# Two attention layers on one core: scores of layer 1 by differences, projections in fewer gaps, a later product on GpSimd, and additions shared with VectorE in one block

## The chip, the core and the metric

The kernel runs on one NeuronCore of a Trainium2 chip. The metric is the device time of one execution in microseconds (us). TensorE is called PE in the profile, its weight loads PEld, VectorE DVE, ScalarE ACT, GpSimd POOL, and SP is the queue that starts most of the transfers.

## The reference, cut to what matters

```python
# x: (2, 256, 64, 64) float32, n = 64*64 = 4096 positions
def layer0(x, w_qkv, w_proj):            # 8 heads of 32 channels
    q, k, v = split(einsum('oc,bcn->bon', w_qkv, x), 3)
    scores = einsum('bhdi,bhdj->bhij', q, k) / sqrt(32)
    out = einsum('bhij,bhdj->bhdi', softmax(scores, axis=-1), v)
    return einsum('oc,bcn->bon', w_proj, out) + x

def layer1(x):                           # one head, keys and values pooled to 1024 positions
    g = maxpool2(conv1x1(x, g_w, g_b))                  # 256 channels x 1024
    theta = conv1x1(x[:, :64], theta_w, theta_b)        #  64 channels x 4096
    phi = maxpool2(conv1x1(x[:, 64:], phi_w, phi_b))    #  64 channels x 1024
    f = softmax(einsum('bcn,bcm->bnm', theta, phi), axis=-1)
    y = einsum('bnm,bcm->bcn', f, g)
    return batchnorm(conv1x1(y, W_w, W_b)) + x
```

Both layers are done in float32 for each of the two batches; each row of a softmax has its largest score subtracted before the exponential.

## The kernel before

**Layer 0.** Four heads are done together, so there are four groups `n` (two batches, two quads of heads), and each has 8 blocks `i` of 512 queries: 32 blocks in all, counted 0 to 31 below. A block has 32 steps `j`, one for each tile of 128 keys. In a step PE makes the scores of the four heads (`score`, L401), and ACT takes the exponential of two heads at a time (L530) into `p`. Even steps start the scores' buffer in PSUM from the negated row maxima (`subtract`, L413: matmuls of `ones_b` with `rows`, in bfloat16); odd steps add the product of the queries with differences of keys (`kd`, `last_kd`) to the scores that still stand there. One step later `weigh` multiplies the probabilities with the values (L425), and DVE adds that to `num` (L436).

**The denominator.** `add` sums the probabilities over the steps: heads 0 and 1 (`p[0]`, 128x1024) on POOL (L449), heads 2 and 3 two steps at a time by accumulating transfers that POOL issues (L457), in turn into two sums. The tiles of `p[0]` come from a pool of 6 buffers, the double tiles of `p[1]` from a pool of 5; ACT can write a tile only when its addition or its transfer is done with it. In the following block `normalize` runs as a generator, a piece a step: a last accumulating transfer at step 2 (L463), the column sums on PE at step 6 (`den`, L475) and their copy by ACT to `r` (L483), two transfers through DRAM from step 7 on (L492, L493), the reciprocal of step 12 (L497), the transfers that spread it over the partitions again (L498, L500), and, five pieces later, at step 17, the product `y = num * r` on POOL (L505). The last block of a batch takes another way: ACT's copy, a reciprocal on DVE (L486) and the product.

**Row maxima.** They are found ahead by a second set of products (`product`, L252), of which two are made at each half step (`advance(maxes)`). DVE reduces them, directly (L264) or together with differences that ACT has cut at zero (L271, L278). This work is one block and some steps ahead: at step 28 of block i it begins with the queries of block i + 2.

**Projections in the gaps.** `during` lists what is projected in a block: for most blocks the queries of block i + 2, and keys and values of chunk i for the next group. One item is made in each of the steps 11, 19 and 27, after that step's `weigh`: `make` reads a chunk of `x` (one buffer), PE multiplies (L195 for q and k, L183 for v), and ACT copies the result out of PSUM (L209, L192). The PSUM tiles for these, for `w` and for the products of the maxima come from one pool of 4 banks (`scratch`); the scores take the other two buffers of two banks each (`scores`). In group 3 there is no next group, and only the queries are left.

**Layer 1.** `project` (L559) ends layer 0 for a batch. `non_local` makes `theta`, `phi` and `g`, folds the output matrix into the values (`wg`), and then goes through 8 blocks `i` of 512 queries with 4 steps `t` of 256 keys. In each step PE makes the scores (L719) and adds the negated maxima (L728, bfloat16), ACT takes the exponential (L732), PE weighs the step before (L687), POOL sums the probabilities (L679, L683), and PE makes a piece of the maxima of later blocks (L655) that DVE reduces (L662). `result` ends a block: column sums (L699), reciprocal (L701) and two pairs of operations on DVE (L703, L706).

Each engine works through its own queue in order; the framework sets the semaphores, and it may let an instruction with ready operands pass others of the program's order.

Of the kernel before, what the change touches and what calls it, by code (L numbers as in the profile page):

```python
# [9 lines left out]
F32 = mybir.dt.float32  # L10
# [12 lines left out]
P = 128  # L23
# [12 lines left out]
def conv_attention(  # L36
# [195 lines left out]

    def during(n, i):
        if i < NI - 2:
            return [("q", n, i + 2), ("k", n + 1, i), ("v", n + 1, i)]
        if i == NI - 2:
            return [("k", n + 1, i), ("k", n + 1, i + 1), ("q", n + 1, 0)]
        return [("v", n + 1, i - 1), ("v", n + 1, i), ("q", n + 1, 1)]


    reduced, cut = None, None
# [119 lines left out]
    def advance(steps, n=1):  # L361
        for _ in range(n):
            next(steps, None)
# [12 lines left out]
    def attend(b, y):  # L376
# [67 lines left out]
        def add(blk, j, p, two):  # L444
            nonlocal added
            if j == 0:
                blk.sums[0] = p[0]
            elif j < NJ - DIRECT:
                added = nc.gpsimd.tensor_add(blk.sums[0], blk.sums[0], p[0])  # L449
            else:  # L450
                blk.last.append(p[0])
            if j % 2:
                n = 1 + j // 2 % 2
                if j < 4:
                    blk.sums[n] = two
                else:
                    nc.gpsimd.dma_start(out=blk.sums[n], in_=two, accum_op=ALU.add)  # L457

        def normalize(blk):
            whole = [1, 2]  # L460
            if (blk.qd, blk.i) != (QUADS - 1, NI - 1):
                with tc.issue_after(added.ins):
                    nc.gpsimd.dma_start(out=blk.sums[1], in_=blk.sums[2], accum_op=ALU.add)  # L463
                whole = [1]
                yield
            den = scratch(f"den_{blk.name}")
            mine = [
                [blk.sums[0], *blk.last],
                [blk.sums[n][:, j] for j in range(2) for n in whole],
            ]  # L470
            for n in range(max(map(len, mine))):
                for h in range(QH):
                    those = mine[h // 2]
                    if n < len(those):
                        nc.tensor.matmul(  # L475
                            den[bass.ts(h, D), :],
                            ones[:, :D],
                            those[n][:, h % 2, :],
                            start=(n == 0),
                            stop=(n == len(those) - 1),  # L480
                        )
            r = work.tile([P, NB], F32, tag="r", name=f"r_{blk.name}", bufs=1)
            nc.scalar.copy(r, den)  # L483
            yield
            if (blk.qd, blk.i) == (QUADS - 1, NI - 1):
                nc.vector.reciprocal(r, r)  # L486
            else:


                flat = [spare.tile([QH, NB], F32, tag=f"flat{a}", name=f"flat{a}_{blk.name}") for a in range(2)]  # L490
                few = work.tile([P, NB // D], F32, tag="few", name=f"few_{blk.name}")
                nc.sync.dma_start(out=flat[0], in_=r[::D, :])  # L492
                nc.sync.dma_start(out=few, in_=flat[0].rearrange("h (c e) -> (h c) e", c=D))  # L493
                for _ in range(5):
                    yield
                with tc.issue_after(reduced.ins):
                    nc.vector.reciprocal(few, few)  # L497
                nc.sync.dma_start(out=flat[1].rearrange("h (c e) -> (h c) e", c=D), in_=few)  # L498
                for h in range(QH):
                    nc.sync.dma_start(  # L500
                        out=r[bass.ts(h, D), :], in_=flat[1][h : h + 1, :].broadcast_to([D, NB])
                    )
                for _ in range(5):
                    yield
            nc.gpsimd.tensor_mul(y[:, blk.qd, bass.ts(blk.i, NB)], blk.num, r)  # L505

        waiting, normal = None, iter(())
        for qd in range(QUADS):
            for i in range(NI):
                blk = Block(qd, i)  # L510
                items = [x for x in during(blk.n, i) if x[1] < len(QUAD)]
                both = [None, None]
                for j in range(NJ):
                    if j % 2 == 0:
                        two = double(f"p_{blk.name}_{j}_1")
                    p = [single(f"p_{blk.name}_{j}_0"), two[:, j % 2]]
                    for pair in range(2):
                        if j % 2 == 0:
                            s = both[pair] = scores(f"s_{blk.name}_{j}_{pair}")
                            subtract(s, pair, blk)  # L520
                            advance(maxes)
                            score(s, pair, blk, j)
                        else:
                            s = both[pair]
                            score(s, pair, blk, j)
                            advance(maxes)
                        with ExitStack() as order:
                            if cut is not None:
                                order.enter_context(tc.issue_after(cut.ins))
                            nc.scalar.activation(p[pair], s, AF.Exp, scale=scale)  # L530
                    if waiting is not None:
                        weigh(*waiting)
                        if j == 0:
                            normal = normalize(waiting[0])
                    add(blk, j, p, two)
                    waiting = blk, j, p
                    if j == 2 or j >= AFTER:
                        advance(normal)
                    if j % 2 == 0:
                        make_rows()  # L540
                        if (i, j) == (0, NJ // 4) and blk.n > 0:
                            differences(blk.n, 1, last_kd)
                    elif j % 8 == 3 and j > 8 and items:
                        advance(make(*items.pop(0)), 9)
        weigh(*waiting)
        return normalize(blk)

# [25 lines left out]
    def non_local(b, y):  # L573
        theta = [double(f"theta_{b}_{t}") for t in range(2)]
        theta = [t[:, a, c, :] for t in theta for a in range(2) for c in range(2)]
        kv = qkv.tile([P, M + NC * M], F32, tag="k", name=f"kv_{b}")
        phi = kv[:, :M]
        wg = kv[:, M:].rearrange("p (m o) -> p m o", o=C)

        gs = qkv.tile([P, NC * (M + 2 * C)], F32, tag="v", name=f"g_{b}")  # L580
        g, gw_sb, ww_sb = (
# [5 lines left out]
        for i in range(NI):  # L587
# [23 lines left out]
            for o in range(NC):  # L611
                for c in range(NC):
                    last_g = nc.tensor.matmul(  # L613
                        s[:, o, :],
                        gw_sb[:, c, bass.ts(o, P)],
                        y[:, c, cols],
                        start=(c == 0),
                        stop=(c == NC - 1),
                    )
                nc.vector.tensor_reduce(  # L620
                    g[:, o, small].rearrange("p (r w) -> p r w", w=WW // 2),
                    pooled(s[:, o, :]),
                    AX.XY,
                    ALU.max,
                )
                nc.vector.tensor_scalar_add(
                    g[:, o, small], g[:, o, small], par[:, G_B + o : G_B + o + 1]
                )

        for t in range(M // P // 2):  # L630
            a = scratch(f"wg_{b}_{t}")
# [81 lines left out]
        for i in range(NI):  # L713
            rows = later
            for t in range(last + 1):
                s = scores(f"f2_{b}_{i}_{t}")
                for h in range(2):
                    half = bass.ts(h, CM)
                    nc.tensor.matmul(  # L719
                        s[:, h, :],  # L720
                        phi[half, bass.ts(2 * t + h, P)],
                        theta[i][half, :],
                        start=True,
                        stop=False,
                    )
                for h in range(2):
                    half = bass.ts(h, CM)
                    nc.tensor.matmul(  # L728
                        s[:, h, :], ones_b[half, :], rows[half, :], start=False, stop=True
                    )  # L730
                p = single(f"p1_{b}_{i}_{t}")
                nc.scalar.activation(p, s, AF.Exp)  # L732
                if waiting is not None:
                    weigh(*waiting)
                waiting = (i, t, p)
                if finish:
                    result(finish.pop())
                if t == last and i + 1 < NI:
                    later = ready[i + 1]()
                advance(maxes1)  # L740
# [84 lines left out]
```

## Time and profile before

| what | us |
|---|---|
| median of three timed runs | 4076.65 (4070.6 to 4076.9) |
| time of the profiled execution | 4069.7 |
| its span, first to last instruction | 4067.9 |
| PE busy in it | 4021.0 (99%) |
| DVE, POOL, ACT busy in it | 2951.8, 2925.8, 2674.3 |

The profile comes from one execution. A line of the timeline gives the start in us, the duration (of a merged line: of all its instructions), engine, source line, operation, the tile written and the tiles read, shapes, the number of instructions, and in brackets the idle time of the engine before it with what ended that. A float32 matmul shows as two records, and matmuls of different rows of the array run at once, so the distance between starts tells more than a duration.

### The profile page before, as it was taken

What the parts mean: (1) busy time and instruction counts of PE and PEld (TensorE: products, weight loads), DVE (VectorE), ACT (ScalarE), POOL (GpSimd) and SP (SyncE); (2) the same over time, 40 slices, a digit from 0 to 9 for tenths busy, and PEclk for the clock granted to TensorE, in tenths of its full rate; (3) what the DMA queues carried; (4) which work ended last, traced back from release to release, by engine and by line L of the source; (5) the groups of instructions that cost most, each with busy time, mean ns of one, the idle gap of its engine ahead of it and who ended that gap; (6) DMA issues with size and microseconds to landing.
All of it is one profiled execution on the core that took longest, in us unless ns stands there. A gap on an engine that the chain in (4) does not pass through costs nothing.

```text
span 4067.9 us, 75415 instructions
## 1 busy us (share of the span) xinstructions
PE 4021.0 (99%) x29712; PEld 1496.4 (37%) x29712; DVE 2951.8 (73%) x5436; ACT 2674.3 (66%) x3329; POOL 2925.8 (72%) x1857
## 2 busy tenths in 40 slices
PE   9999999999999999999999999999999999999998
PEld 4333333333333333333333333333333333332333
DVE  5877777788777778774457778777888888882434
ACT  5777777777777777741147777777677777776121
POOL 0888888778878888761457878887888888888143
PEclk9999999999999999999999999999999999999999
DMA  1677777777777777780027777878777777777200
GB/s 59 143 161 162 154 163 161 163 160 164 161 159 164 165 159 161 165 195 0 21 52 156 163 165 160 168 159 173 160 164 161 162 159 161 160 156 162 74 16 26
DMA packets 113380, 569.35 MB, mean 140 GB/s; under 512 B 20232, under 2 KB 22024, under 8 KB 51840
## 3 DMA queue, kind: packets, MB, share of 16 engines
q0 software_dynamic: 68832, 501.25, 60.1%
q1 hardware_dynamic: 42928, 62.10, 5.1%
q8 instruction: 232, 3.80, 0.4%
q10 hardware_dynamic: 1264, 1.19, 0.1%
q14 instruction: 124, 1.02, 0.1%
HBM read 54.39 MB, written 8.88 MB: 16 GB/s over the span
## 4 chain that ended last, share of the span: by engine, by line
PE 88%; DMA 5%; DVE 2%; POOL 2%; issue 2%; ACT 1%; SPq 0%; POOLq 0%; DVEq 0%; ACTq 0%
PE ps L252 27%; PE w L425 22%; PE s L401 16%; PE y L687 5%; PE s L413 5%; DMA p<-p 3%; PE v L183 2%; PE q L195 2%; PE k L195 1%; PE den L475 1%; POOL p L449 1%; DMA flat<-few 1%; PE g L613 1%; DVE r L701 1%; PE f L655 1%
## 5 line engine op out<-in xcount | busy, mean ns | idle before, releaser
L449 POOL TENSOR_TENSOR p<-p,p 128x1024 f32<-128x1024 f32 x960 | 2365.5, 2464 | 446.2 <-ACT p L530 308.3
L252 PE MATMUL ps<-k,q 32*128 32x512 f32 x6232 | 2120.7, 619 | 2.3 <-DVE part L278 1.0
L530 ACT ACTIVATE p<-s 128x1024 f32<-128x1024 f32 x2048 | 1987.7, 1024 | 138.8 <-PE ps L252 46.1
L264 DVE TENSOR_REDUCE part<-ps 128x1 f32<-128x512 f32 x2136 | 1374.5, 686 | 115.6 <-PE ps L252 72.0
L425 PE MATMUL w<-p,v 128*32 128x512 f32 x8192 | 1092.7, 605 | 0.0
L278 DVE CUSTOM_DVE_ANT_0 ps<-ps,over 128x512 f32<-128x512 f32 x980 | 683.7, 700 | 553.0 <-PE ps L252 297.1
L401 PE MATMUL s<-q,k 32*128 32x512 f32 x4096 | 1020.7, 593 | 0.0
L271 ACT ACTIVATE over<-ps 128x512 f32<-128x512 f32 x916 | 547.4, 598 | 558.1 <-PE ps L252 550.6
L252 PEld LDWEIGHTS ps<-k,q 32*128 32x128 f32 x6232 | 785.9, 184 | 260.3 <-DVE num L436 84.1
L436 DVE TENSOR_TENSOR num<-num,w 128x512 f32<-128x512 f32 x992 | 671.9, 677 | 81.4 <-PE w L425 78.0
L252 PE MATMUL ps<-kd,q 32*128 32x512 f32 x1056 | 567.5, 642 | 1.0 <-POOL kd L214 0.7
L401 PE MATMUL s<-q,last_kd 32*128 32x512 f32 x2048 | 516.2, 616 | 9.6 <-ACT p L530 9.5
L401 PE MATMUL s<-q,kd 32*128 32x512 f32 x2048 | 513.3, 615 | 6.0 <-ACT p L530 6.0
L252 PE MATMUL ps<-last_kd,q 32*128 32x512 f32 x904 | 481.2, 639 | 1.5 <-POOL last_kd L214 1.5
L425 PEld LDWEIGHTS w<-p,v 128*32 128x32 f32 x8192 | 161.5, 108 | 778.9 <-ACT over L271 684.8
L457 POOL DMA_DIRECT2D p<-p x448 | 390.4, 871 | 42.1 <-ACT p L530 39.2
L413 PE MATMUL s<-rows,ones_b 32*128 32x512 bf16 x2048 | 395.2, 380 | 0.2 <-ACT p L530 0.2
L401 PEld LDWEIGHTS s<-q,k 32*128 32x128 f32 x4096 | 365.1, 184 | 5.8 <-issue 1.4
L413 PEld LDWEIGHTS <-ones_b 32*128 32x128 bf16 x2048 | 131.1, 91 | 500.6 <-PE ps L252 230.6
L401 PEld LDWEIGHTS s<-q,kd 32*128 32x128 f32 x2048 | 174.5, 184 | 228.0 <-ACT p L530 202.1
L401 PEld LDWEIGHTS s<-q,last_kd 32*128 32x128 f32 x2048 | 172.2, 184 | 233.8 <-ACT p L530 216.1
L687 PE MATMUL y<-p,kv 128*128 128x512 f32 x512 | 240.0, 608 | 3.7 <-DVE r L701 3.7
(104 smaller groups left out, 2235.0 us busy)
## 6 DMA issues: line engine op xcount, KB each, us to landing
p<-p POOLq DMA_DIRECT2D x478, 1024.0 KB, 7.5
x_k<-in_x_dram SPq DMA_DIRECT2D x32, 512.0 KB
x_q<-in_x_dram SPq DMA_DIRECT2D x30, 512.0 KB
x_res<-in_x_dram SPq DMA_DIRECT2D x16, 512.0 KB
out_dram<-z SPq DMA_DIRECT2D x16, 512.0 KB
r<-flat SPq DMA_DIRECT2D x120, 64.0 KB
x_v<-in_x_dram SPq DMA_DIRECT2D x6, 512.0 KB
wqk_sb<-in_wqk_dram ACTq DMA_DIRECT2D x1, 512.0 KB
```

The source lines that it names most:

```text
L252: nc.tensor.matmul(ps, q[n, i][bass.ts(h, D), bass.ts(g, P)], keys[bass.ts(h, D), :], start=True, stop=True,)
L264: reduced = nc.vector.tensor_reduce(part[:, g, h, j : j + 1], ps, AX.X, ALU.max)
L271: cut = nc.scalar.activation(over, ps, AF.Relu)
L278: reduced = nc.vector.tensor_tensor_reduce(out=ps, in0=ps, in1=over, scale=1.0, scalar=LEAST, op0=ALU.add, op1=ALU.max, accum_out=part[:, ...
L401: nc.tensor.matmul(s[:, t, :], kj[bass.ts(h, D), :], q[blk.n, blk.i][bass.ts(h, D), :], start=False, stop=True, skip_group_check=j % 2 == 1,)
L413: nc.tensor.matmul(s[:, t, :], ones_b[bass.ts(h, D), :], rows[blk.rows][bass.ts(h, D), :], start=True, stop=False,)
L425: nc.tensor.matmul(w[bass.ts(h, D), :], v[blk.n][:, keys(j), h, :], p[h // 2][:, h % 2, :], start=True, stop=True,)
L436: nc.vector.tensor_add(blk.num, blk.num, w)
L449: added = nc.gpsimd.tensor_add(blk.sums[0], blk.sums[0], p[0])
L457: nc.gpsimd.dma_start(out=blk.sums[n], in_=two, accum_op=ALU.add)
L530: nc.scalar.activation(p[pair], s, AF.Exp, scale=scale)
L687: nc.tensor.matmul(acc[i][o], wg[:, 2 * t + j, bass.ts(o, P)], p[:, j, :], **edge)
```

## The change

- `during` returns groups, and a group is made in one gap. For i < 6 keys and values of a chunk are made together at step 15, and the queries of block i + 2 at step 27. For i = 6 and 7 there are three groups of one item at steps 11, 19 and 27, as before.
- In `add`, in the last block of the last group (block 31), the probabilities `p[0]` of odd steps are added on DVE to the tile of step 1; POOL adds those of even steps.
- In `normalize` the product on POOL comes 13 pieces after the reciprocal instead of 5: at step 25 instead of 17.
- In layer 1 a block keeps one score tile in PSUM over its four steps. Step 0 starts it from `phi` and the maxima; steps 1 to 3 add the product of `theta` with differences of `phi` that lie 256 columns apart. The differences (`dphi`, 128x768) are made once a batch on POOL and stand behind `wg` in the same tile.

```diff
     def during(n, i):
         if i < NI - 2:
-            return [("q", n, i + 2), ("k", n + 1, i), ("v", n + 1, i)]
+            return [[("k", n + 1, i), ("v", n + 1, i)], [("q", n, i + 2)]]
         if i == NI - 2:
-            return [("k", n + 1, i), ("k", n + 1, i + 1), ("q", n + 1, 0)]
-        return [("v", n + 1, i - 1), ("v", n + 1, i), ("q", n + 1, 1)]
+            return [[("k", n + 1, i)], [("k", n + 1, i + 1)], [("q", n + 1, 0)]]
+        return [[("v", n + 1, i - 1)], [("v", n + 1, i)], [("q", n + 1, 1)]]
...
             if j == 0:
                 blk.sums[0] = p[0]
+            elif j % 2 and (blk.n, blk.i) == (len(QUAD) - 1, NI - 1):
+
+                if j == 1:
+                    blk.last.append(p[0])
+                else:
+                    nc.vector.tensor_add(blk.last[0], blk.last[0], p[0])
             elif j < NJ - DIRECT:
                 added = nc.gpsimd.tensor_add(blk.sums[0], blk.sums[0], p[0])
...
-                for _ in range(5):
+                for _ in range(13):
                     yield
             nc.gpsimd.tensor_mul(y[:, blk.qd, bass.ts(blk.i, NB)], blk.num, r)
...
-                items = [x for x in during(blk.n, i) if x[1] < len(QUAD)]
+                groups = during(blk.n, i)
+                items = [[x for x in g if x[1] < len(QUAD)] for g in groups]
...
-                    elif j % 8 == 3 and j > 8 and items:
-                        advance(make(*items.pop(0)), 9)
+                    elif items and j in ((15, 27), (11, 19, 27))[len(groups) - 2]:
+                        for item in items.pop(0):
+                            advance(make(*item), 9)
...
-        kv = qkv.tile([P, M + NC * M], F32, tag="k", name=f"kv_{b}")
+
+        kv = qkv.tile([P, M + NC * M + M - 2 * P], F32, tag="k", name=f"kv_{b}")
         phi = kv[:, :M]
-        wg = kv[:, M:].rearrange("p (m o) -> p m o", o=C)
+        dphi = kv[:, (1 + NC) * M :]
+        wg = kv[:, M : (1 + NC) * M].rearrange("p (m o) -> p m o", o=C)
...
+        nc.gpsimd.tensor_sub(dphi, phi[:, 2 * P :], phi[:, : M - 2 * P])
...
             for t in range(last + 1):
-                s = scores(f"f2_{b}_{i}_{t}")
+                if t == 0:
+                    s = scores(f"f2_{b}_{i}")
                 for h in range(2):
                     half = bass.ts(h, CM)
+                    keys = phi if t == 0 else dphi[:, 2 * P * (t - 1) :]
                     nc.tensor.matmul(
                         s[:, h, :],
-                        phi[half, bass.ts(2 * t + h, P)],
+                        keys[half, bass.ts(h, P)],
                         theta[i][half, :],
-                        start=True,
-                        stop=False,
+                        start=(t == 0),
+                        stop=(t > 0),
+                        skip_group_check=t > 0,
                     )
                 for h in range(2):
                     half = bass.ts(h, CM)
-                    nc.tensor.matmul(
-                        s[:, h, :], ones_b[half, :], rows[half, :], start=False, stop=True
-                    )
+                    if t == 0:
+                        nc.tensor.matmul(
+                            s[:, h, :], ones_b[half, :], rows[half, :], start=False, stop=True
+                        )
```

## The prediction

> **What bounds the kernel now.** I read the page first: PE is busy for 99% of the span at a granted clock of 9 tenths or more in every slice, and the chain that ended last runs over PE for 88%.
>
> ```profile
> PE 4021.0 (99%) x29712; PEld 1496.4 (37%) x29712; DVE 2951.8 (73%) x5436; ACT 2674.3 (66%) x3329; POOL 2925.8 (72%) x1857
> PE 88%; DMA 5%; DVE 2%; POOL 2%; issue 2%; ACT 1%; SPq 0%; POOLq 0%; DVEq 0%; ACTq 0%
> ```
>
> So an edit counts only if it takes matmul time off PE or ends a time in which PE waits for another engine. DMA and POOL have 7% of the chain: those are the waits to look for. I then took the distance between exponentials, step by step, in all 32 blocks. An even and an odd step together take 6.12 us, the column sums add 1.7 us at step 6, a projection about 2 us. A block without disturbance lasts 106.0 us; the disturbances are regular enough to be priced one by one, from the timelines below.
>
> **Projections: k and v together at step 15, q at step 27.** Timeline of PE at step 27, with v in the gap (block 5), with q in the gap (block 6, where the old code has a q there too), and with nothing in it (block 24):
>
> ```profile
> 719.27 1.06 PE L425 MATMUL w<-p,v 128*32 128x512 f32 x8
> 720.27 2.05 PE L183 MATMUL v<-wv_sb,x_k 128*128 128x128 f32 x16
> 722.25 0.39 PE L413 MATMUL s<-rows,ones_b 32*128 32x512 bf16 x2
> 724.39 0.64 PE L425 MATMUL w<-p,v 128*32 128x512 f32 x4
> ...
> 825.43 1.06 PE L425 MATMUL w<-p,v 128*32 128x512 f32 x8
> 826.43 1.98 PE L195 MATMUL q<-x_q,wqk_sb 128*128 128x512 f32 x4
> 828.35 0.39 PE L413 MATMUL s<-rows,ones_b 32*128 32x512 bf16 x2
> 829.09 0.69 PE L252 MATMUL ps<-kd,q 32*128 32x512 f32 x1
> 831.22 0.64 PE L425 MATMUL w<-p,v 128*32 128x512 f32 x4
> ...
> 3039.41 1.06 PE L425 MATMUL w<-p,v 128*32 128x512 f32 x8
> 3043.17 0.64 PE L425 MATMUL w<-p,v 128*32 128x512 f32 x4
> ```
>
> From one w to the next it takes 5.12 us with v, 5.79 with q and 3.76 with nothing. With v the first product of the new maxima (ps<-kd) starts at 722.26, beside the rows; with q it starts 0.74 us after them, at 829.09. It needs the very q that the gap made: step 28 begins the maxima of block i + 2, and ACT copies q only from 828.45 to 829.04. Blocks 7, 14 and 22 show the same loss. So putting q where v was costs 5.79 - 5.12 = 0.67 us.
>
> In return q leaves step 11 and k leaves step 19 (1.92 us each on PE, 1201.04 to 1202.96 for a q), and k enters step 15 with v. A lone gap pays twice for PE's change from four heads to full rows and back: the first matmul of each kind starts its successor 0.1 us later (0.53 instead of 0.43 us). One gap fewer saves 2 x 0.1 = 0.2 us. I take 0.15 for it: k's tile in PSUM must not hold v back. Four banks serve k, v, the last w and two products, and DVE needs 0.68 us for each of these, while k's matmuls last 1.7 us; so v finds a bank. If it had to wait for k's copy that would be 0.8 us a block.
>
> Sum: 18 blocks (groups 0 to 2, i < 6) at 0.67 - 0.15 = +0.52, +9.4 us. In group 3 six blocks move a q alone from step 11 (1.92) to step 27 (5.79 - 3.76 = 2.03): +0.11 each, +0.7. **Together +10 us**, bounds +6 and +14 (+24 if v waits for k's copy).
>
> The transfers move too. SP issues the load for k right behind the matmuls that free the x buffer: now those of step 27, some 48 us before step 15. The q load follows v at step 15, 12 steps (about 37 us) before its use. The old k had 24.5 us (issue 349.05, use 373.56) and PE did not wait. On SP the q load may now stand ahead of L498 and L500 and delay the reciprocal's way back until step 15; only the product at step 25 needs that.
>
> **The product at step 25.** Timelines of POOL and ACT in block 10:
>
> ```profile
> 1216.58 1.28 POOL L505 TENSOR_TENSOR y<-num,r 128x512 f32<-128x512 f32 x1 [5.25 <-DMA r<-flat]
> ...
> 1226.19 1.02 ACT L530 ACTIVATE p<-s 128x1024 f32<-128x1024 f32 x1 [2.08 <-DMA p<-p]
> ```
>
> POOL stands still for 5.25 us because the product waits for the transfers of r. Queued behind it are the accumulating transfer of two steps and the additions; six microseconds late they free the tiles of p late, and ACT, then PE (1.55 us here) run dry. The idle time is 3.3 to 5.7 us in the blocks 1 to 30, 8.65 in block 31; half of the blocks swallow it, half do not. The excess of steps 15 to 23 over a clean block, in us: 1.0, 0.9, 0.2, 1.7, 0.8, 0.5, 0.6, 1.0, 1.0 in blocks 3, 4, 9, 10, 11, 14, 18, 21, 22, and 1.0, 0.1, 1.6, 0.4, 0.5, 0.5 in blocks 24 to 28 and 30: 11.8 together. The last r lands 2 us after its issue, at about step 16, nine steps before the new place, so the wait goes. What is late next: at step 25 POOL has 1.27 us for the product and about 1.3 us of small operations for the maxima soon after, 2.6 us against the 6 that did no harm in half of the blocks; two steps need 2 x 2.46 + 0.87 = 5.8 us of POOL's 6.1. **-11.8 us**, bounds -5 and -12. `num` and `r` stay in use 8 steps longer, but their buffers are next wanted a block later.
>
> **Block 31.** There are no maxima left in it, two steps take PE 5.41 us, and POOL needs 5.63 (the distance of its additions); it is the bound there and never catches up:
>
> ```profile
> 3711.03 1.28 POOL L505 TENSOR_TENSOR y<-num,r 128x512 f32<-128x512 f32 x1 [8.65 <-DMA r<-flat]
> ...
> 3719.21 1.94 ACT L530 ACTIVATE p<-s 128x1024 f32<-128x1024 f32 x2 [5.00 <-DMA p<-p]
> ```
>
> The block's steps exceed 5.41 a pair plus column sums by 10.7 us: 7.7 in steps 14 and 15, the rest in steps 6 to 9. The change takes away the wait of 8.65 and 15 of 30 additions, which leaves POOL 3.3 us in 5.41. On DVE 15 additions of 128x1024 appear; the nearest row is L566 with 1.22 us, so 18 us in a block where DVE is busy for 21 of 96. I take **-9 us**, bounds -5 and -10.7, as POOL still waits 3.35 us for a transfer at step 2. The tile of step 1 stays taken for the block: four of the six remain for p[0], and DVE frees each within about 2 us.
>
> A rule speaks against this edit. The Trainium skill, page "SBUF — State Buffer", section "Who interferes with whom", says that a VectorE instruction with two SBUF inputs and a GpSimd instruction that reads SBUF block one another for a whole instruction. The trace has such a meeting in layer 1: L706 takes 0.74 us alone and 0.80 to 0.86 where an addition of POOL overlaps it. By the trace the sum above stands. By the rule an addition on DVE could wait 2.46 us more; with two additions to num that makes 1.22 + 2.46 + 2 x 0.69 = 5.1 us of 5.41, and the sum stays as well.
>
> The column sums of block 31 then need not wait for a late transfer (PE idle 0.67 us before the den matmuls at 3786.16): **-0.7 us**.
>
> **Layer 1.** PE at step 1 of a block, behind the column sums of the block before and a piece of the maxima:
>
> ```profile
> 1928.12 1.02 PE L719 MATMUL f<-theta,kv 64*128 64x512 f32 x4
> 1928.98 0.38 PE L728 MATMUL f<-rows_l,ones_b 64*128 64x512 bf16 x2
> 1929.29 1.12 PE L687 MATMUL y<-p,kv 128*128 128x512 f32 x2
> 1930.68 1.55 PE L687 MATMUL y<-p,kv 128*128 128x512 f32 x3 [0.26 <-DVE r L701]
> ```
>
> The pair L728 costs 0.31 - 0.10 = 0.21 us (the two run at once, and the change of rows comes anyway). It goes in 3 of 4 steps: 2 x 8 x 3 = 48 pairs, 10.1 us. But in step 1 of all blocks but the first, y waits for the bank that the reciprocal frees (0.26 us); that time is set by DVE, and PE arrives 0.21 earlier to wait 0.21 longer. 14 of the 48 gain nothing: 34 x 0.21 = **-7.1 us**, bounds -10 and 0. The new dependency, scores onto a tile that ACT still reads, lies behind other work: between two steps' scores PE has 4.3 us of weighing and maxima, the exponential ends 1.2 us after the scores. POOL's subtraction of 128x768 is 3/4 of an addition of 2.46, 1.85 us, between the last phi (1888.5) and the first maxima reduced by DVE (1894.4): nothing.
>
> **Sum.** +10 - 11.8 - 9 - 0.7 - 7.1 = -18.6 us. The profiled execution, to which these belong, took 4069.7 and would take 4051; the three timed runs have a median 7 us above it (4076.65), which gives 4058. I name 4057.
>
> **Rivals.** (1) The waits move instead of ending: POOL is nearly full in any block (5.8 of 6.1 us), so ACT's waits for p come back after step 25, and block 31 stays bound by its transfers. Then the two large gains are gone: +10 - 0.7 - 7.1 = +2, 4079. Against it: 15 of 30 blocks bore a delay of 6 us without loss. (2) Slower: q's copy queues behind exponentials. ACT was idle for 1.84 us before the copy at 828.45; if in the new order the two exponentials of a step stand ahead (1.93 us for a pair), the new maxima and all scores behind them on PE wait that much in 24 blocks: +46 us, 4104. It decides above (18.6 + 8.2)/24 = 1.1 us a block. Against it: every q at step 27 in the old trace shows 0.74. (3) The framework draws q's projection ahead and its copy is ready in time: 24 x 0.74 = 18 us less, 4040. Against it: the same six cases.
>
> **Chances.** A difference under 0.2% (8.2 us) cannot be told from none. Forecast 0.72, its own range 4043 to 4072 from the bounds above; rival 1 0.12, rival 2 0.08, rival 3 0.08. Faster: 0.68 of the forecast and rival 3, 0.76; same: 0.04 and rival 1, 0.16; slower: rival 2, 0.08. The range 4040 to 4074 leaves out rivals 1 and 2.
>
> **What would show it.** Step 27 with q: first ps 0.74 us after the rows in all blocks with i < 6; POOL's product at step 25 with no idle time ahead of it, and no waits of ACT for "DMA p<-p" at steps 18 to 21; block 31 near 88 us; L728 x32 instead of x128, and y's wait for the reciprocal near 0.47 us. A wait of ACT for p after step 25, or a q that arrives over 1.1 us late, would prove me wrong.

## The result, and the profile after

The changed kernel takes 4071.47 us (median of 22 runs, 4066.07 to 4078.89) against 4076.78 before (22 runs, 4070.60 to 4084.58): ratio 0.9989, 95% interval 0.9983 to 0.9995. That is 5.3 us less, where 19.7 were forecast. The kernel before, measured anew beside each of the three later series of runs, had medians of 4077.73 to 4079.24, and each ratio below goes by the one beside it. The profiled execution after took 4072.2 us (span 4070.4) and is a typical one; the one before (4069.7) had been shorter than all 22 timed runs, so the two traces are compared step by step, not by their spans.

The page of the changed kernel, in the lines that answer to those shown of before, and one more (POOL's row has 945 additions, 15 fewer):

```profile
PE 4021.6 (99%) x29616; PEld 1495.2 (37%) x29616; DVE 2974.8 (73%) x5451; ACT 2673.8 (66%) x3329; POOL 2892.5 (71%) x1844
PE 89%; DMA 5%; DVE 2%; POOL 1%; issue 1%; ACT 1%; SPq 0%; POOLq 0%; DVEq 0%; ACTq 0%
L455 POOL TENSOR_TENSOR p<-p,p 128x1024 f32<-128x1024 f32 x945 | 2331.0, 2467 | 444.5 <-ACT p L537 308.1
```

PE has 96 matmuls fewer and is as busy as before, and the chain still runs 5% over DMA: waits for transfers have not gone.

**The product stayed where it was.** POOL's timeline in block 10, at the place shown of before:

```profile
1209.87 2.36 POOL L455 TENSOR_TENSOR p<-p,p 128x1024 f32<-128x1024 f32 x1 [0.56 <-ACT p L537]
1216.90 1.26 POOL L511 TENSOR_TENSOR y<-num,r 128x512 f32<-128x512 f32 x1 [4.67 <-DMA r<-flat]
1218.10 0.87 POOL L463 DMA_DIRECT2D p<-p  x1
...
3525.14 1.28 POOL L511 TENSOR_TENSOR y<-num,r 128x512 f32<-128x512 f32 x1 [6.83 <-DVE part L264]
3526.36 0.87 POOL L463 DMA_DIRECT2D p<-p  x1
```

It runs at 50.1 us of block 10 (before: 52.5), still behind 4 to 7 us of idle POOL; the last two lines are block 29, with 6.83. Counting the additions that POOL issues ahead of it gives 13 in each of blocks 1 to 30 in both traces; the source says 25 now and said 17 before. The framework's order of POOL's queue was never the order of the source.

For block 29 the profile names a reduction of DVE as what ended the wait, because it came last by semaphore; SP issued the four transfers of r only from 3521.49 to 3523.20 there, so r was late in this block too.

What the wait does in block 29, on ACT (the longest such wait of blocks 1 to 30), and on PE behind it:

```profile
3530.09 1.02 ACT L537 ACTIVATE p<-s 128x1024 f32<-128x1024 f32 x1
3534.29 1.02 ACT L537 ACTIVATE p<-s 128x1024 f32<-128x1024 f32 x1 [3.18 <-DMA p<-p]
```

```profile
3535.37 0.70 PE L401 MATMUL s<-q,last_kd 32*128 32x512 f32 x2 [2.66 <-ACT p L537]
```

The transfer that POOL issued late lands late, ACT has no tile to write, and PE idles 2.66 us. Block 29 lasts 107.4 us; clean ones of its kind last 102.8.

The idle time is not the whole price. PE's next work is slower; the product of probabilities and values before and after the wait, and a product of the maxima behind it:

```profile
3530.57 1.06 PE L425 MATMUL w<-p,v 128*32 128x512 f32 x8
3536.44 1.50 PE L425 MATMUL w<-p,v 128*32 128x512 f32 x8
3537.88 1.22 PE L252 MATMUL ps<-last_kd,q 32*128 32x512 f32 x1
```

The profile shows a granted clock of 0.50 for 3.4 us there (3536.9 to 3540.3), which costs some 1.7 us; with the 2.66 us of idle time that is nearly the whole excess of the block. In block 31 the clock stands at 0.50 for 6.8 us in both traces (some 3.4 us lost; before, behind 4.90 us of idle PE), and in the changed kernel for another 3.4 us, behind 2.15 us. So part of the 7.7 us of steps 14 and 15 that the prediction reads from the trace of before is the slower clock. Not every such wait brings it: 2.71 us of idle PE in block 19 of run 5 did not.

**Queries at step 27.** PE in block 5, from one w to the next:

```profile
720.71 1.06 PE L425 MATMUL w<-p,v 128*32 128x512 f32 x8
721.71 1.98 PE L195 MATMUL q<-x_q,wqk_sb 128*128 128x512 f32 x4
723.62 0.39 PE L413 MATMUL s<-rows,ones_b 32*128 32x512 bf16 x2
724.37 0.69 PE L252 MATMUL ps<-kd,q 32*128 32x512 f32 x1
726.50 1.06 PE L425 MATMUL w<-p,v 128*32 128x512 f32 x8
```

726.50 - 720.71 = 5.79 us, the forecast to the hundredth; the first new product starts 0.75 us after the rows. A clean block of groups 0 to 2 lasts 106.5 us instead of 106.0.

**Layer 1.** The groups of the changed kernel (count | busy, mean ns | idle time ahead):

```profile
L698 PE MATMUL y<-p,kv 128*128 128x512 f32 x512 | 240.0, 608 | 6.4 <-DVE r L712 6.4
L743 PE MATMUL f<-rows_l,ones_b 64*128 64x512 bf16 x32 | 6.1, 376 | 0.0
L639 POOL TENSOR_TENSOR kv<-kv 128x768 f32<-128x768 f32 x2 | 3.6, 1803 | 117.3 <-DVE kv L617 117.3
```

96 matmuls of rows are gone, y's wait for the reciprocal has grown from 3.7 to 6.4 us (0.26 to 0.46 each), and the subtraction costs 1.8 us of an idle POOL. From the start of block 15 to that of block 16, with all of layer 1 of the first batch between them, it takes 394.2 us instead of 397.8.

**Block 31** takes 94.8 us up to its last step, 1.4 less than before; near 88 had been expected.

### The profile page after: what moved, and what is told of

It is laid out like the page before. It is cut to its first block, busy times and chain, and to the rows that moved or that the text cites. A ratio compares the mean times of both kernels' runs of the same rounds, so it can differ in the third digit from the quotient of the medians.

```text
span 4070.4 us, 75211 instructions
## 1 busy us (share of the span) xinstructions
PE 4021.6 (99%) x29616; PEld 1495.2 (37%) x29616; DVE 2974.8 (73%) x5451; ACT 2673.8 (66%) x3329; POOL 2892.5 (71%) x1844
## 4 chain that ended last, share of the span: by engine, by line
PE 89%; DMA 5%; DVE 2%; POOL 1%; issue 1%; ACT 1%; SPq 0%; POOLq 0%; DVEq 0%; ACTq 0%
PE ps L252 27%; PE w L425 23%; PE s L401 17%; PE y L698 5%; PE s L413 5%; DMA p<-p 3%; DMA flat<-few 2%; PE q L195 2%; PE den L481 1%; PE k L195 1%; PE proj L567 1%; PE g L623 1%; PE v L183 1%; DVE r L712 1%; PE f L666 1%
## 5 line engine op out<-in xcount | busy, mean ns | idle before, releaser
L455 POOL TENSOR_TENSOR p<-p,p 128x1024 f32<-128x1024 f32 x945 | 2331.0, 2467 | 444.5 <-ACT p L537 308.1
L401 PE MATMUL s<-q,k 32*128 32x512 f32 x4096 | 1038.0, 594 | 0.0
```

Of the source, the lines that this page charges most:

```text
L401: nc.tensor.matmul(s[:, t, :], kj[bass.ts(h, D), :], q[blk.n, blk.i][bass.ts(h, D), :], start=False, stop=True, skip_group_check=j % 2 == 1,)
```

## The experiments

Theory A: the place in POOL's queue decides, and the edit of the pieces did not change it. Theory D: q made one step ahead of the maxima that read it costs 0.67 us a block. Two further theories on layer 1 (F) and block 31 (G) stand with their runs.

**1. The product's edit undone.**

```diff
# against the changed kernel
-                for _ in range(13):
+                for _ in range(5):
                     yield
```

> The changed kernel with the product's edit undone (5 pieces instead of 13 behind the reciprocal). Theory A, the product never moved: in the old and in the changed trace it stands behind 13 additions of its block in POOL's queue, so the edit is without effect; time 4071.5 as the changed kernel, product still behind 13 additions with 4 to 8 us of idle POOL ahead of it. Rival B, the edit did move something and its gain was lost elsewhere: 5 to 12 us slower than the changed kernel, and another place in the queue.

Measured: 4072.61 us (4068.28 to 4076.58), ratio to before 0.9984 (0.9975 to 0.9993); the changed kernel has 0.9989. The product stands behind 13 additions again, and 4 in block 31, and POOL issues the same instructions in the same order in both traces. The edit has no effect that can be told; rival B falls.

**2. and 3. The product bound to a place.**

```diff
# against the changed kernel; and against the kernel before, with range(13) there too
-            nc.gpsimd.tensor_mul(y[:, blk.qd, bass.ts(blk.i, NB)], blk.num, r)
+            if (blk.qd, blk.i) == (QUADS - 1, NI - 1):
+                nc.gpsimd.tensor_mul(y[:, blk.qd, bass.ts(blk.i, NB)], blk.num, r)
+            else:
+                with tc.issue_after(added.ins):
+                    nc.gpsimd.tensor_mul(y[:, blk.qd, bass.ts(blk.i, NB)], blk.num, r)
```

`added` is the addition that POOL got last, and `tc.issue_after` makes the framework put the product behind it in the queue.

> The changed kernel with the product bound behind the addition of step 25 in POOL's queue. Theory A (only the queue's place counts): POOL's idle time ahead of the product under 0.5 us, no waits of ACT for 'DMA p<-p' at steps 18 to 21; blocks 4, 11, 20 and 24 to 30 lose about 14 us of excess and block 31 about 5.5 us of its stall at steps 14 and 15, in all some 17 to 20 us: 4053. Rival C (POOL is nearly full, the waits only move to later steps): 4068 to 4072.

> The kernel before with nothing but the product bound behind the addition of step 25 in POOL's queue. Theory A: the 11.8 us of excess in blocks 1 to 30 go, and some 4 of the 7.7 us of steps 14 and 15 of block 31, where POOL stays the bound with 30 additions: 4061. Rival C: 4074 to 4077, with waits of ACT for p at steps behind 25.

Measured: the changed kernel with it 4047.63 us (4045.64 to 4048.26), ratio 0.9922 (0.9910 to 0.9935); the kernel before with nothing but it 4046.32 us (4046.21 to 4047.27), ratio 0.9921 (0.9909 to 0.9933). The second, POOL in block 11, in its timeline, and then the row of the product among its groups:

```profile
1244.82 2.35 POOL L449 TENSOR_TENSOR p<-p,p 128x1024 f32<-128x1024 f32 x1 [0.57 <-ACT p L534]
1247.13 1.28 POOL L509 TENSOR_TENSOR y<-num,r 128x512 f32<-128x512 f32 x1
1248.35 0.87 POOL L457 DMA_DIRECT2D p<-p  x1
```

```profile
L509 POOL TENSOR_TENSOR y<-num,r 128x512 f32<-128x512 f32 x30 | 38.4, 1280 | 0.0
```

The thirty products have no idle time ahead of them, 25 additions stand before each, and the excess of steps 15 to 23 is nowhere. Block 31 takes 86.1 us instead of 96.2. The span is 22.4 us shorter than in the trace of before: block 31 starts 11.9 us earlier and takes 10.1 less. The price of 11.8 for blocks 1 to 30 is met; the 9 us of block 31 had been priced for this wait and the additions on DVE together, and the wait alone brings more than that. Rival C falls: POOL holds the pace although nearly full. Against the median the gain is 30 us, because the profiled execution of before was a short one. The scatter goes with the wait: the eight kernels with the product bound spread over 0.6 to 3.0 us in 4 or 5 runs each, the others over 8 to 14 us in 7 to 22.

**4. The product bound to step 17.** The kernel before with its 5 pieces and the same binding.

> The kernel before with its 5 pieces, the product bound behind the addition of step 17. Theory A with the landing of r at step 16 or 17: POOL waits under 1.5 us ahead of the product, the excess of blocks 1 to 30 goes almost wholly and block 31 keeps a part: 4047 to 4052. If nine steps of room are needed: 4060 or more.

Measured: 4045.94 us (4045.32 to 4046.34), ratio 0.9918 (0.9903 to 0.9933). The row of the product among POOL's groups:

```profile
L509 POOL TENSOR_TENSOR y<-num,r 128x512 f32<-128x512 f32 x30 | 38.4, 1281 | 0.0
```

The program's old step would have done, once it was the queue's place; four additions of room (17 instead of 13, in block 31 17 instead of 9) end the wait, block 31 included (85.3 us).

**5. The changed kernel with the old gaps.** `during`, `items` and the test of the step are those of before.

> The changed kernel with the old gaps (q at step 11, k at 19, v at 27). Theory D (q's copy beside the first new maxima costs 0.67 us a block, the saved gap returns 0.15): 18 blocks go from 106.5 back to 106.0 us, group 3 is 0.1 us a block shorter, 10 us less on PE's path: 4061. If the pauses of the double gap at step 15 also help POOL over the product's wait, some of the waits at steps 18 to 21 return in groups 0 to 2 (6 to 8 us): 4067 to 4069. Rival E (the new gaps cost nothing): 4071.5 or slower.

Measured: 4067.00 us (4064.13 to 4072.89), ratio 0.9972 (0.9961 to 0.9982). It is 4.5 us faster than the changed kernel, not 10, and the second case expected is seen: clean blocks are back at 106.0 us, but blocks 3, 4, 5, 10, 11, 19, 20 have waits again (107.3 to 108.9), where the changed kernel lengthens only 4 and 20 of these by over 1 us (and 11 by 0.4). The traces show how: in sixteen blocks of groups 0 to 2 (i < 6, with a product in them) the addition of step 15 begins on average 6.1 us after the end of its exponential with the double gap and 6.0 without; that of step 16, behind the gap, 2.8 us after it with the gap and 5.9 without. So the pause of the double gap let POOL catch up a part of the product's wait.

In group 3 it is the other way round. There the change only takes q out of step 11, so no projection is made ahead of the product; POOL is idle for 4.9 to 6.8 us before it in blocks 24 to 30, with the old gaps for 3.2 to 5.8. Against the same gaps with the product bound (run 2, and run 8 for the old gaps), blocks 24 to 30 are 12.3 us longer in the changed kernel's trace and 5.7 with the old gaps; blocks 1 to 14 and 17 to 23 are 4.5 and 15.2 longer. With the wait itself gone, the parts can be measured one by one. Runs 6 to 9 come from another series, on another chip of the same kind, than run 3; of differences near 1 us, the lengths of blocks in the traces are better evidence than the medians.

**6. The new gaps alone, on the kernel before with the product bound.** The diff is that of the change to `during`, `items` and the test of the step.

> The kernel before with the product bound behind the addition of step 25 (4046.3), and the new gaps alone of the change. Theory D: 18 blocks at +0.52 and 6 at +0.1, 10 us slower: 4056, blocks at 106.5 instead of 106.0 us. Rival E (gaps are neutral): 4046.

Measured: 4060.02 us (4058.91 to 4060.38), ratio 0.9955 (0.9943 to 0.9968), 13.7 us slower than run 3. Rival E falls. Clean blocks last 106.5 us, those of group 3 102.8 instead of 102.7, and block 31 starts 8.5 us later; then it takes 90.0 us instead of 86.1, 3.9 more in steps 6 to 9. The second part had not been foreseen: there PE's column sums and ACT wait for transfers (the timeline of ACT in block 31 of this kernel):

```profile
3686.27 1.02 ACT L535 ACTIVATE p<-s 128x1024 f32<-128x1024 f32 x1 [1.87 <-DMA p<-p]
...
3694.98 1.94 ACT L535 ACTIVATE p<-s 128x1024 f32<-128x1024 f32 x2 [2.23 <-DMA p<-p]
```

Behind them the granted clock is 0.50 for 3.4 us, some 1.7 of the 3.9. Why these waits are longer with the new gaps is not shown.

**7. The same gaps in the other order**, q at step 15, k and v at step 27.

```diff
# against run 6
-            return [[("k", n + 1, i), ("v", n + 1, i)], [("q", n, i + 2)]]
+            return [[("q", n, i + 2)], [("k", n + 1, i), ("v", n + 1, i)]]
```

> The kernel before with the product bound, and the new groups in the other order: q alone at step 15, k and v together at step 27. Theory D (q must not be made in the step ahead of the maxima that read it): step 27 without q's wait, one gap fewer, so 0.15 us a block less than the old gaps in 18 blocks: 4043.5, blocks at 105.9. Rival H (a double gap costs by itself, wherever it is): 4050 or more, as slow as with q at step 27.

Measured: 4045.43 us (4042.71 to 4045.72), ratio 0.9919 (0.9905 to 0.9932): 14.6 us faster than run 6 with the same two gaps. Clean blocks last 105.8 us, 0.2 less than with three gaps, and step 27 has no wait for q. PE in block 5, at step 27:

```profile
714.77 1.06 PE L425 MATMUL w<-p,v 128*32 128x512 f32 x8
715.77 1.99 PE L195 MATMUL k<-x_k,wqk_sb 128*128 128x512 f32 x4
717.59 1.95 PE L183 MATMUL v<-wv_sb,x_k 128*128 128x128 f32 x16
719.47 0.39 PE L413 MATMUL s<-rows,ones_b 32*128 32x512 bf16 x2
719.47 0.69 PE L252 MATMUL ps<-kd,q 32*128 32x512 f32 x1
```

The first new product starts with the rows. Theory D holds and rival H falls. Of the 2.7 us of one gap fewer 0.9 remain in the median; block 31, at 88.3 us here instead of 86.1, can account for the rest (its clock is 0.50 for 3.4 us, some 1.7).

**8. Layer 1 alone, on the kernel before with the product bound.**

> The kernel before with the product bound, and layer 1's differences alone. Theory F: 34 of 48 pairs of rows save 0.21 us and 14 turn into a longer wait of y for the reciprocal, -7.1 us: 4039, that wait 0.47 instead of 0.26 us. Rival (all 48 pairs count): -10.1, 4036. Rival (the scores wait for the exponential): 4046 or slower.

Measured: 4039.96 us (4039.43 to 4040.05), ratio 0.9906 (0.9893 to 0.9920): -6.4 us. From block 15 to block 16 it takes 394.2 us instead of 397.8, and y waits 6.4 us in all instead of 3.7. Theory F holds; the rival of all 48 pairs and that of waiting scores fall.

**9. The additions on DVE alone, on the same base.**

> The kernel before with the product bound, and the additions of odd steps on DVE in block 31 alone. Theory G (most of what these additions were priced at was the product's wait): block 31 goes from 86.1 to about 85 us, -1 to -2 us: 4045. Rival (POOL is the bound of block 31 with 5.63 us of 5.41): block 31 at 82 us, 4042.

Measured: 4045.06 us (4044.07 to 4046.69), ratio 0.9919 (0.9906 to 0.9933): -1.3 us, and block 31 takes 84.5 us instead of 86.1. Theory G holds: POOL's excess over 5.41 us a pair is worth little in one block. In every kernel with these additions and the product bound, block 31 takes 84.5 to 84.8 us, also with the new gaps; without them it varied from 85.3 to 90.0.

**10. What the runs point to.** The changed kernel with the product bound (run 2) and the groups in the other order (run 7).

> The changed kernel with the product bound behind the addition of step 25 and the groups in the other order (q alone at step 15, k and v at step 27). If the parts add up: 4047.6 less the 10 us of q at step 27 and 2.7 of one gap fewer, 4035.

Measured: 4033.04 us (4032.57 to 4034.30), ratio to before 0.9886 (0.9870 to 0.9903), 38.4 us less than the changed kernel. The parts add up.

## Why the prediction was wrong

**The step that failed** is "so the wait goes" under "The product at step 25". The price of that wait, 11.8 us in blocks 1 to 30, was right (run 3), but the change does not take it away: POOL is still idle for 4.4 to 7.1 us before the product. I read the place of the product from the source (step 17, now 25). The trace of before had the other answer: 13 additions ahead, not 17. With an order that leaves the source's, an edit that only moves a line in the source need not move the instruction. I had noted that the framework may let instructions pass one another, and did not count. That the change doesn't do what it says was not among the rivals. Why the framework puts the product behind 13 additions is not shown.

**Block 31** (-9 us) hung on the same step: 7.7 of its excess was the product's wait of 8.65 us and the slower clock behind it, and the change keeps the wait (7.98 us, now behind 4 additions instead of 9). Binding the product alone takes 10.1 us off the block (run 3); the additions on DVE, once the product is bound, take another 1.6 off it (run 9). With both, the block takes 84.8 us (run 2), 10 less than in the changed kernel.

**The gaps** (+10 us) held in their mechanism and their price: 5.79 us from w to w, 106.5 us a block, +8.5 us up to block 31. What the sum left out is block 31, 3.9 us longer with the new gaps alone: +13.7 in all (run 6). In the changed kernel over half of the 10 came back, since the double gap gave POOL time to catch up (run 5). One reading was off without consequence: the load of k is issued 64 us before its use (296.1 to 360.2 in block 2), not 48. The sum had added the gaps and the waits as if they were independent, and they were so only with the waits gone.

**Layer 1** (-7.1 us) held: -6.4 (run 8), and 2 x 3.7 by the traces. So did the reason for leaving out 14 pairs.

**The column sums at the end** (-0.7): the idle time before them is gone from the trace of the changed kernel, but 0.7 us can't be told apart in the times.

**The account of the 5.3 us.** With the product bound the changed kernel and the one before are 1.3 us apart, 4047.6 and 4046.3: layer 1 and DVE's additions give about what the gaps take. What the product's wait costs is the distance to the bound versions: 4076.8 - 4046.3 = 30.5 us before and 4071.5 - 4047.6 = 23.9 after. The gain is this difference, 6.6 less 1.3, and rests on a smaller share of waits reaching PE, not on any part of the sum that I had made; a double gap beside the wait helped groups 0 to 2 by luck. The two costs of the wait come from different series; by the ratios, which go by the kernel before of the same series, they are near 32 and 27, again some 5 apart. That 4071.5 lies within the stated range of 4040 to 4074 does not support the sum either: its two largest gains did not come.

**The rivals.** The first is the one whose time came nearest (4079, where 4071.5 was measured), but by a wrong way: the waits did not move to later steps, they stayed. The second and third did not occur: with q at step 27 the first new product starts 0.74 us after the rows in every block from 0 to 29.

**The rule on two SBUF inputs**, weighed in the prediction (the Trainium skill, "SBUF — State Buffer", "Who interferes with whom"), is seen in the changed kernel's block 31. DVE's addition, and POOL's beside it, each from the timeline of its engine:

```profile
3729.09 2.83 DVE L453 TENSOR_TENSOR p<-p,p 128x1024 f32<-128x1024 f32 x1 [3.04 <-ACT p L537]
```

```profile
3728.18 2.65 POOL L455 TENSOR_TENSOR p<-p,p 128x1024 f32<-128x1024 f32 x1
```

Alone the addition on DVE takes 1.23 us. Here it begins 0.91 us after POOL's and ends 1.09 us after POOL's end at 3730.83. Every other addition of the block that begins while one of POOL's is running also ends 1.08 or 1.09 us after it: two that take 1.92 and 2.38 us, and eight that meet only its last 0.2 us and take 1.28 to 1.31. Whatever the overlap, all but some 0.14 us of DVE's work (1.23 less 1.09) comes after POOL's end. The rows with L706 that I had set against the rule overlap POOL by only 0.25 to 0.32 us, and so show only its last bit. As reckoned there, it changes nothing in the sum.

## What to carry to other kernels

Before pricing a move of an instruction, find its place in the engine's queue in the trace: count what its engine issues ahead of it, and compare that with the source. If they differ, a moved line proves nothing, and the place has to be bound to an instruction. An engine that is busy for 72% and not the bottleneck can cost the bottleneck 30 us in 4077 when one instruction at the head of its queue waits 5 us for a transfer, and a scatter of the runs that is wider than that of similar kernels is a hint to such a wait. Projections are best made a few steps ahead of their readers, not in the gap before.

## What the runs showed of the hardware that I had not expected

Blocking between VectorE and GpSimd shows as a longer instruction, not as idle time: 1.23 us became 1.92, 2.38 and 2.83 where an addition of POOL was already running. A wait of PE of 2.66 us lengthened its block by 4.6, with the granted clock at 0.50 for the 3.4 us behind it. And 3.3 to 5.7 us of idle POOL a block, harmless in half of the blocks of one profiled execution, cost 30 us in the median of the timed runs: that the wait costs a varying share from run to run, by how late its transfers land, would fit the scatter, but only single executions were traced, so this reason is argued, not shown.
